# Attention stage of a decoder layer: order of the values, of one load of keys and of the query rows

## The chip, the cores and the metric

One core of a Trainium2 chip runs the whole layer in one launch. The time is device microseconds of that core; three runs of the kernel before gave 2487.85, 2491.16 and 2492.6 us. The core has TensorE (PE; PEld is its weight loads), VectorE (DVE), ScalarE (ACT), GpSimd (POOL) and SyncE (SP), which work side by side and wait for each other only where data or buffers demand it. In this kernel each engine runs its instructions in the order in which the program writes them.

## The reference

`x` is 16 sequences of 112 rows by 1024, the context 16 of 375 rows. Three blocks, each followed by a layer norm without weights:

```
x = layernorm(x + ((topk_zeroed(silu(x @ Wg.T)) * (x @ Wu.T)) @ Wd.T))  # the half with the smallest size zeroed
q = x @ Wq                        # 32 heads of 32
k, v = ctx @ Wk, ctx @ Wv         # 8 heads of 32, each shared by 4 heads of q
p = softmax(q @ k.T * 32 ** -0.5)
x = layernorm(x + (p @ v) @ Wo)
x = layernorm(x + bf16(x) @ bf16(dequantize(qweight, qscale, qzeros)).T)
```

## The kernel before

The first 1746 us compute the first block and the keys and values of the context; rows of `x` after the first norm go to DRAM as `x1_d`, keys and values as `k_d` and `v_d`. The rest, `attention_and_ffn` (L1247), is what the change touches.

Attention is cut into 128 **units** (L1541): a sequence `b` (16), a half `c` of the key heads (2) and a position `r` in the group of four heads that share one key head (4). A unit handles four heads at once. The loop at L1619 writes, for each unit `n`, these steps in this order:

- at every fourth unit the load of the keys for the next four units (L1621), by SP's queue;
- `scores(n)` (L1304): four matmuls of 32 rows into two PSUM tiles (`sc0`, `sc1`, one buffer each), two maxima on DVE (L1323), four exponentials on ACT (L1325). The next unit's scores need the PSUM tiles back from the exponentials;
- `normalize(n - 1)` (L1331): reciprocals on DVE, a product on POOL (L1334);
- `square(n - 2)` (L1338): a transposition in squares of 32 on DVE (L1345), and after each second unit 16 transfers of 96 KB that lay the weights out for the values, 11 on SP's queue and 5 on POOL's (L1359);
- one piece of other matmul work (L1630 to L1634): either a piece of a tail, or, where none is ready, a chunk of the queries of a coming group of two sequences (`Queries.chunk`, L1235: 8 products of 224 columns, copied out by ACT). A chunk is also taken ahead of tail pieces when its group comes near (`due`, L1630);
- at every even unit the values of the pair of units that ended five units before (`attend`, L1601, which calls `values`, L1361): 12 products, with one PSUM tile `po` per four units, copied to `aT` by ACT after its second pair, and then the load of the next values by SP;
- rows of a coming group (L1638 to L1647): `Queries.rows` (L1223) transposes 112 rows by 1024 on PE and ACT copies them into `x1T`; two sequences make a group, the second two units after the first, since both pass through one buffer `xr` that `fetch` (L1218) loads by ACT's queue. The eight chunks of the group come after both;
- `lights(n)` (L1597): steps of tails that hang on a unit: statistics, `normed` (L1450: normalization by ACT, a cast to bf16 by DVE), `turn` (L1455: transposes on PE, a copy by ACT), `store`.

A **tail** is a block of 128 rows whose attention is complete: `project` (L1403) multiplies by the output weights, in two halves of columns, each in two pieces; an add on DVE (L1415), statistics, the cast, the turn, and `packed` (L1463), the product with the dequantized weights, whose result POOL adds (L1474). Its rows `x1` (L1400) lie in one of three buffers. In both kernels the pieces of tails start after the values that complete their rows.

Before the loop (L1544 to L1551) SP issues the first keys, two loads of values, and the output weights in 16 transfers of 256 KB. After the loop (L1653 on) the last values, tails and the store follow in an order written out by hand.

The rule that says when the rows of the next group are due:

```python
due = (turned // GB - 1) * per_group if turned % GB == 0 else when + 2
if not asked and turned < B and n >= due:
```

`turned` counts sequences whose rows are transposed, `asked` holds the chunks that wait, `per_group` is 16 units, `GB` is 2 and `LAG` is 5.

Of the kernel before, what the change touches and what calls it, by code (L numbers as in the profile page):

```python
# [10 lines left out]
F32 = mybir.dt.float32  # L11
# [11 lines left out]
P = 128  # L23
B, S, D = 16, 112, 1024
NT = B * S
TT = NT // P
KC = D // P
# [10 lines left out]
GB = 2  # L38
# [24 lines left out]
LAG = 5  # L63
# [1146 lines left out]
class Queries:  # L1210
# [4 lines left out]
        self.pool = ctx.enter_context(tc.tile_pool(name="q_work", bufs=1, side="right"))  # L1215
        self.x1T, self.qT, self.xr = {}, {}, {}

    def fetch(self, queue, g, bb):  # L1218

        self.xr[g, bb] = self.pool.tile([S, D], F32, tag="xr", name=f"xr_{g}_{bb}")  # L1220
        queue.dma_start(self.xr[g, bb], self.x1_d[ds((g * GB + bb) * S, S), :])

    def rows(self, g, bb):  # L1223
# [23 lines left out]
def attention_and_ffn(nc, tc, ident, ident_b, negh, x1_d, k_d, v_d, queries, wf_sb, wo, out):  # L1247
# [16 lines left out]
    with ExitStack() as ctx:  # L1264
# [6 lines left out]
        ld = ctx.enter_context(tc.tile_pool(name="a_ld", bufs=2))  # L1271
# [21 lines left out]
        def load_keys(b, c):  # L1293
            keys[b, c] = ld.tile([P, SK], F32, tag="kT", name=f"kT_{b}_{c}")
            nc.sync.dma_start(keys[b, c], k_d[:, c, ds(b * SK, SK)])

        def load_values(b, c):
            vals[b, c] = ld.tile([P, NKP, P], F32, tag="v", name=f"v_{b}_{c}")
            nc.sync.dma_start(
                vals[b, c],  # L1300
                v_d[ds(b * SK, SKP), ts(c, P)].rearrange("(k p) n -> p k n", p=P),
            )

        def scores(n):  # L1304

            b, c, r = units[n]
            kt = keys[b, c]
            q = queries.qT[b // GB]
            pr = probs[:, n % 3]
            sums = small.tile([P, 4], F32, tag="sums", name=f"sums_{n}", bufs=4)  # L1310

            sc, nmax = [], []
            for h in range(2):
                sc.append(ps_s.tile([P, 2, 512], F32, tag=f"sc{h}", name=f"sc_{n}_{h}"))
                nmax.append(small.tile([P, 2], F32, tag=f"nmax{h}", name=f"nmax_{n}_{h}", bufs=2))
            for i in range(4):
                nc.tensor.matmul(  # L1317
                    sc[i // 2][:, i % 2, :SK],
                    q[ts(i, HD), c * REP + r, ds(b % GB * (GT - P), P)],
                    kt[ts(i, HD), :], start=True, stop=True,  # L1320
                )
            for h in range(2):
                nc.vector.tensor_reduce(nmax[h], sc[h][:, :, :SK], AX.X, ALU.max, negate=True)  # L1323
            for i in range(4):
                nc.scalar.activation(  # L1325
                    pr[:, i, :SK], sc[i // 2][:, i % 2, :SK], AF.Exp,
                    bias=nmax[i // 2][:, i % 2 : i % 2 + 1], accum_out=sums[:, i : i + 1],
                )
            return sums

        def normalize(n, sums):  # L1331
            pr = probs[:, n % 3, :, :SK]
            nc.vector.reciprocal(sums, sums)  # L1333
            nc.gpsimd.tensor_tensor(  # L1334
                pr, pr, sums.unsqueeze(2).to_broadcast([P, 4, SK]), ALU.mult
            )
# [205 lines left out]
        n_units = len(units)  # L1542
        per_group = n_units // (B // GB)
        load_keys(0, 0)  # L1544
        load_values(0, 0)
        load_values(0, 1)
        by_head = wo.rearrange("p (c i) n -> p i c n", i=4)
# [6 lines left out]

        asked, behind, light = deque((0, mc) for mc in range(EARLY, KC)), deque(), {}
        turned, fetched, when = GB, GB, 0
        sums, tails = {}, {}
        done = soon = now = 0

# [13 lines left out]
        def piece(n, halves=(0, 1)):  # L1573

            nonlocal now
            now = n
            if opened:
                close()
                return True
            i = next((i for i, (first, *_) in enumerate(behind) if first <= n), None)  # L1580
            if i is None:
                return False
            _, tail, part = behind[i]
            del behind[i]
            if part < 2:
                tail.project(part, 0)
                opened.append([tail, part, 0])
            else:
                tail.packed(halves)
                if halves == (0,):  # L1590
                    behind.append((n, tail, part))
                    return True
                at(n + 1, tail.stats)
                at(n + 2, tail.store)
            return True

        def lights(n):  # L1597
            for step in light.pop(n, []):
                step()

        def attend(m):  # L1601

            nonlocal soon, done
            b, c, r = units[m]
            while r == 3 and ((b + 1) * S - 1) // P - 3 in aTs:
                piece(n)
            values(m)
            if r == 3 and m // 4 + 2 < 2 * B:
                load_values(b + 1, c)
            if r == 3 and c == 0:  # L1610
                soon = (b + 1) * S // P
            while (c, r) == (1, 3) and (done + 1) * P <= (b + 1) * S:
                if done not in tails:
                    tails[done] = Tail(done)
                tail = tails.pop(done)
                behind.extend((n + 1, tail, i) for i in range(2))
                done += 1

        for n in range(n_units):  # L1619
            b, c, r = units[n]  # L1620
            if n % 4 == 1 and n // 4 + 1 < 2 * B:  # L1621
                load_keys(*divmod(n // 4 + 1, 2))
            sums[n] = scores(n)
            if n:
                normalize(n - 1, sums.pop(n - 1))
            if n > 1:
                square(n - 2)

            now = n
            due = asked and n >= asked[0][0] * per_group + asked[0][1] - 2  # L1630
            if due or (not piece(n) and asked):
                queries.chunk(*asked.popleft())
            if n == 0:
                queries.chunk(*asked.popleft())  # L1634
            if n > LAG and (n - LAG) % 2:
                attend(n - LAG)

            due = (turned // GB - 1) * per_group if turned % GB == 0 else when + 2  # L1638
            if not asked and turned < B and n >= due:
                when = n  # L1640
                queries.rows(turned // GB, turned % GB)
                turned += 1
                if turned % GB == 0:
                    asked.extend((turned // GB - 1, mc) for mc in range(KC))
            if fetched == turned < B:
                queries.fetch(nc.scalar, fetched // GB, fetched % GB)
                fetched += 1  # L1647
            lights(n)
            if done + len(tails) < soon and Tail.live < 3:
                tails[done + len(tails)] = Tail(done + len(tails))  # L1650


        n = n_units  # L1653
# [34 lines left out]
def kernel(  # L1688
# [37 lines left out]
    with AsWritten(nc, tc) as order:  # L1726
        with ExitStack() as psum:
# [30 lines left out]
            for mc in range(EARLY):  # L1758
                queries.chunk(0, mc)
        attention_and_ffn(nc, tc, ident, ident_b, negh, x1_d, k_d, v_d, queries, wf_sb, wo, out)  # L1760


# [46 lines left out]
```

## Time and profile before

| | us |
|---|---|
| three runs, median | 2491.16 |
| profiled execution, its own time | 2492.81 |
| its span in the profile | 2491.0 |
| first scores start (unit 0) | 1746.67 |
| last scores start (unit 127) | 2429.37 |
| last values start | 2457.35 |

PE counts as busy for 98% of the span, DVE 54%, POOL 45%, ACT 31%. The mean granted clock of TensorE is 0.991. Matmuls are pipelined and their ends are modelled, so a busy PE need not run at its best. In a line of the timeline the numbers are start, length and, after the shape, how many instructions were merged; a bracket gives the idle time of that engine before it and what ended it. In the table of stages each engine has its busy time and its count of instructions; after them stand the granted clock of TensorE, the busy share of the 16 DMA engines and GB/s.

### The profile page before, as it was taken

What the parts mean: (1) busy time and instruction counts of PE and PEld (TensorE: products, weight loads), DVE (VectorE), ACT (ScalarE), POOL (GpSimd) and SP (SyncE); (2) the same over time, 40 slices, a digit from 0 to 9 for tenths busy, and PEclk for the clock granted to TensorE, in tenths of its full rate; (3) what the DMA queues carried; (4) which work ended last, traced back from release to release, by engine and by line L of the source; (5) the groups of instructions that cost most, each with busy time, mean ns of one, the idle gap of its engine ahead of it and who ended that gap; (6) DMA issues with size and microseconds to landing.
All of it is one profiled execution on the core that took longest, in us unless ns stands there. A gap on an engine that the chain in (4) does not pass through costs nothing. (4 is left out here: it accounts for less than half of the span.)

```text
span 2491.0 us, 31025 instructions
## 1 busy us (share of the span) xinstructions
PE 2438.1 (98%) x9746; PEld 1373.1 (55%) x9746; DVE 1349.6 (54%) x2258; ACT 782.3 (31%) x1844; POOL 1108.7 (45%) x1086
## 2 busy tenths in 40 slices
PE   9999999999999999999999999999899999999997
PEld 4456666544445666666964444444655555565543
DVE  0283587698862333332311523167667777777773
ACT  0352354345520111111110000000555655555652
POOL 1756233244253242332310000033578888888883
PEclk9999999999999999999999999999999999999998
DMA  9567876855454978676765233275877777787763
GB/s 358 197 244 267 294 265 233 259 177 182 141 179 134 305 233 262 202 224 205 244 203 163 77 117 102 73 237 182 199 194 189 199 193 199 186 207 190 194 183 104
DMA packets 331082, 498.12 MB, mean 200 GB/s; under 512 B 49849, under 2 KB 264994, under 8 KB 329122
## 3 DMA queue, kind: packets, MB, share of 16 engines
q1 hardware_dynamic: 260770, 381.93, 49.9%
q0 software_dynamic: 23168, 61.66, 8.4%
q10 hardware_dynamic: 46976, 52.50, 6.7%
q8 instruction: 80, 1.31, 0.2%
q14 instruction: 88, 0.72, 0.1%
HBM read 311.64 MB, written 83.63 MB: 159 GB/s over the span
## 5 line engine op out<-in xcount | busy, mean ns | idle before, releaser
L1334 POOL TENSOR_TENSOR probs<-probs,sums 128x1500 f32<-128x1500 f32 x128 | 344.2, 2691 | 118.0 <-DVE sums L1333 102.8
L1325 ACT ACTIVATE probs<-sc,nmax 128x375 f32<-128x375 f32 x512 | 286.7, 572 | 230.0 <-DVE nmax L1323 224.2
L1323 DVE TENSOR_REDUCE nmax<-sc 128x2 f32<-128x750 f32 x256 | 228.6, 931 | 127.3 <-PE sc L1317 126.7
L1011 PE MATMUL m<-wd,h 128*128 128x512 f32 (+1 forms) x616 | 265.1, 592 | 0.0
L698 ACT ACTIVATE ja<-a,to 128x1824 int8<-128x1824 f32 x98 | 177.8, 1814 | 211.5 <-DVE to L758 198.2
L470 POOL TENSOR_TENSOR c<-c,us 128x384 f32<-128x384 f32 (+1 forms) x84 | 89.0, 1060 | 346.0 <-DVE c L418 148.0
L1345 DVE STREAM_TRANSPOSE squares<-probs 128x1536 f32<-128x1536 f32 x128 | 224.2, 1751 | 26.8 <-DMA weights<-squares 11.4
L406 PE MATMUL pu_A<-u,xe 128*128 128x384 f32 (+2 forms) x768 | 237.9, 453 | 0.0
L406 PE MATMUL pu_S<-u,xe 128*128 128x384 f32 (+2 forms) x768 | 237.8, 452 | 0.0
L406 PE MATMUL pu_S<-u,xl 128*128 128x384 f32 (+2 forms) x768 | 230.0, 453 | 0.0
L1240 PE MATMUL bank<-x1T,wq_sb 128*128 128x224 f32 x1008 | 209.9, 362 | 0.0
L1240 PEld LDWEIGHTS bank<-x1T,wq_sb 128*128 128x128 f32 x1008 | 188.0, 192 | 34.4 <-issue 30.7
L1011 PEld LDWEIGHTS m<-wd,h 128*128 128x128 f32 (+1 forms) x616 | 116.8, 190 | 146.1 <-issue 144.4
L1409 PE MATMUL bank<-wo_sb,aT 128*128 128x512 f32 x416 | 192.0, 605 | 0.0
L406 PEld LDWEIGHTS pu_S<-u,xe 128*128 128x128 f32 x768 | 145.8, 190 | 76.0
L1359 POOL DMA_DIRECT2D weights<-squares x320 | 178.9, 565 | 8.9 <-issue 4.4
L406 PEld LDWEIGHTS pu_S<-u,xl 128*128 128x128 f32 x768 | 143.7, 190 | 70.9
L406 PEld LDWEIGHTS pu_A<-u,xe 128*128 128x128 f32 x768 | 141.6, 190 | 65.6 <-issue 0.4
L502 ACT COPY hT<-pt 128x384 f32<-128x384 f32 (+1 forms) x112 | 47.7, 426 | 363.5 <-PE pt L498 331.4
L1141 POOL TENSOR_TENSOR y<-y,c 128x512 f32<-128x512 f32 x7 | 10.0, 1423 | 326.9 <-DMA zi<-in_qz_dram 326.8
L242 PE MATMUL pg<-wg_sb,xp 128*128 128x456 f32 (+1 forms) x384 | 149.9, 553 | 2.1 <-DMA wg_sb<-in_wg_dram 2.1
L1317 PE MATMUL sc<-kT,qT 32*128 32x375 f32 x1024 | 139.3, 533 | 11.0 <-ACT probs L1325 6.0
(204 smaller groups left out, 3391.3 us busy)
## 6 DMA issues: line engine op xcount, KB each, us to landing
weights<-squares SPq DMA_DIRECT2D x704, 96.0 KB
h<-hT_d SPq DMA_DIRECT2D x56, 640.0 KB
weights<-squares POOLq DMA_DIRECT2D x320, 96.0 KB, 3.5
xe<-in_xT_dram SPq DMA_DIRECT2D x48, 512.0 KB
xe<-xs_d SPq DMA_DIRECT2D x48, 512.0 KB
xl<-xs_d SPq DMA_DIRECT2D x48, 512.0 KB
u<-in_wg_dram SPq DMA_DIRECT2D x32, 688.0 KB
a<-s_d SPq DMA_DIRECT2D x14, 1376.0 KB
```

The lines of the kernel that those rows point to most:

```text
L242: nc.tensor.matmul(pg[:, :w], xts[t][:, kc, :], wg_sb[:, kc, ds(off, w)], start=(kc == 0), stop=(kc == KC - 1),)
L406: nc.tensor.matmul(m, a(n), k[:, n, :], start=(n == 0), stop=(n == KH - 1))
L698: nc.scalar.activation(ja, a[:, NV:], AF.Sign, bias=to, scale=-1.0, accum_out=st["sgn"])
L1011: self.nc.tensor.matmul(bank, a[:r, k, :], b(k)[:r], start=(k == 0), stop=(k == HK - 1),)
L1240: nc.tensor.matmul(pq[:, :GT], self.wq_sb[:, kc, ts(mc, P)], self.x1T[g][:, kc, :], start=(kc == 0), stop=(kc == KC - 1),)
L1317: nc.tensor.matmul(sc[i // 2][:, i % 2, :SK], q[ts(i, HD), c * REP + r, ds(b % GB * (GT - P), P)], kt[ts(i, HD), :], start=True, stop=True,)
L1323: nc.vector.tensor_reduce(nmax[h], sc[h][:, :, :SK], AX.X, ALU.max, negate=True)
L1325: nc.scalar.activation(pr[:, i, :SK], sc[i // 2][:, i % 2, :SK], AF.Exp, bias=nmax[i // 2][:, i % 2 : i % 2 + 1], accum_out=sums[:, i : i ...
L1334: nc.gpsimd.tensor_tensor(pr, pr, sums.unsqueeze(2).to_broadcast([P, 4, SK]), ALU.mult)
L1345: nc.vector.transpose(sq[:, :, n % 2].rearrange("p k (i f) -> p k i f", f=Q), probs[:, n % 3].rearrange("p i (k f) -> p k i f", f=Q),)
L1359: queue.dma_start(wt[ts(m, Q), :, j], by_part[ts(j, Q), :, m])
L1409: nc.tensor.matmul(self.pp, aT[:, h, r, :], wo_sb[:, h * REP + r, ts(i, 512)], start=(h == 0 and r == 0), stop=(h == 1 and r == REP - 1),)
```

## The change

Four things, all in the attention stage. The second keys are loaded right after the first, ahead of the 16 output-weight transfers, and no longer at unit 1. The values of a pair come one unit later, at odd units, right behind that unit's scores and ahead of its piece of other work, instead of at the end of the even unit. The second sequences of the groups 1 and 2 (numbers 3 and 5) have their rows loaded before the loop, into two of the three `x1` buffers, which no tail uses yet; their rows may be transposed in the same unit as the first sequence's. The rows of a group are due one unit earlier than before, and the rule may run twice in a unit.

```diff
-    def fetch(self, queue, g, bb):
-
-        self.xr[g, bb] = self.pool.tile([S, D], F32, tag="xr", name=f"xr_{g}_{bb}")
+    def fetch(self, queue, g, bb, place=None):
+
+        if place is None:
+            place = self.pool.tile([P, D], F32, tag="xr", name=f"xr_{g}_{bb}")
+        self.xr[g, bb] = place[:S]
         queue.dma_start(self.xr[g, bb], self.x1_d[ds((g * GB + bb) * S, S), :])
...
         load_keys(0, 0)
+        load_keys(0, 1)
         load_values(0, 0)
...
         turned, fetched, when = GB, GB, 0
+        apart = {GB + 1, 2 * GB + 1}
+        for i in sorted(apart):
+            place = ld.tile([P, D], F32, tag="x1", name=f"xr_{i}", bufs=3)
+            queries.fetch(nc.scalar, i // GB, i % GB, place)
...
-            if n % 4 == 1 and n // 4 + 1 < 2 * B:
+            if n % 4 == 1 and 1 < n // 4 + 1 < 2 * B:
                 load_keys(*divmod(n // 4 + 1, 2))
             sums[n] = scores(n)
+            if n > LAG + 1 and n % 2:
+                attend(n - LAG - 1)
...
-            if n > LAG and (n - LAG) % 2:
-                attend(n - LAG)
-
-            due = (turned // GB - 1) * per_group if turned % GB == 0 else when + 2
-            if not asked and turned < B and n >= due:
-                when = n
-                queries.rows(turned // GB, turned % GB)
-                turned += 1
+
+            for _ in range(2):
                 if turned % GB == 0:
-                    asked.extend((turned // GB - 1, mc) for mc in range(KC))
-            if fetched == turned < B:
-                queries.fetch(nc.scalar, fetched // GB, fetched % GB)
-                fetched += 1
+                    due = (turned // GB - 1) * per_group - 1
+                else:
+                    due = when + (0 if turned in apart else 2)
+                if not asked and turned < B and n >= due:
+                    when = n
+                    queries.rows(turned // GB, turned % GB)
+                    turned += 1
+                    if turned % GB == 0:
+                        asked.extend((turned // GB - 1, mc) for mc in range(KC))
+                if fetched == turned < B:
+                    if fetched not in apart:
+                        queries.fetch(nc.scalar, fetched // GB, fetched % GB)
+                    fetched += 1
```

## The prediction

> **What bounds the kernel now.** I read the page first, then the busy time of the engines by stage, then the matmul timeline of the attention stage unit by unit (a unit is one pass of the loop at L1619), then DVE and ACT beside it, and last the chain of waits at the end.
>
> ```profile
> PE 2438.1 (98%) x9746; PEld 1373.1 (55%) x9746; DVE 1349.6 (54%) x2258; ACT 782.3 (31%) x1844; POOL 1108.7 (45%) x1086
> ```
>
> TensorE is the bound over the whole, so only what makes it idle or slow can be won. The stages (start and end, length, busy time of PE, PEld, DVE, ACT and POOL, granted clock, DMA share, GB/s) are units 0 to 20, units 21 to 126, and the end:
>
> ```profile
> 1746.67:1858.69 112.02, 100.15 (x664) 72.42 (x665) 72.45 (x86) 60.66 (x198) 76.14 (x66) 0.91 0.80 195
> 1858.69:2429.37 570.68, 563.62 (x3612) 316.18 (x3609) 438.09 (x552) 330.41 (x1016) 474.08 (x442) 1.00 0.76 194
> 2429.37:2491.00 61.63, 44.05 (x194) 18.55 (x192) 23.38 (x41) 17.08 (x30) 21.17 (x25) 0.89 0.38 102
> ```
>
> The loss sits at both ends of the attention stage, where the clock is also below 1. The same view around the low clock:
>
> ```profile
> 1766.99:1770.40 3.41, 0.00 (x0) 0.00 (x0) 0.00 (x0) 0.00 (x0) 3.41 (x6) 1.00 1.05 222
> 1784.05:1787.46 3.41, 2.71 (x16) 1.37 (x16) 3.40 (x5) 2.32 (x10) 3.17 (x2) 1.00 1.09 258
> 1787.46:1794.29 6.83, 6.63 (x19) 4.61 (x20) 3.67 (x5) 4.46 (x16) 6.80 (x7) 0.50 1.08 240
> 1838.66:1848.90 10.24, 6.12 (x40) 3.13 (x40) 4.33 (x5) 2.86 (x9) 6.94 (x7) 0.50 1.08 247
> ```
>
> After a thin 3.4 us the clock is halved for 3.4 us or a few times that. The timeline of PE shows what is thin:
>
> ```profile
> 1762.96 3.29 PE L1240 MATMUL bank<-x1T,wq_sb 128*128 128x224 f32 x16
> 1770.44 1.75 PE L1317 MATMUL sc<-kT,qT 32*128 32x375 f32 x8 [4.18 <-DMA kT<-k_d]
> ...
> 1780.99 0.91 PE L1317 MATMUL sc<-kT,qT 32*128 32x375 f32 x8
> ...
> 1784.25 0.90 PE L1317 MATMUL sc<-kT,qT 32*128 32x375 f32 x4 [0.91 <-ACT probs L1325]
> 1785.36 0.90 PE L1317 MATMUL sc<-kT,qT 32*128 32x375 f32 x4 [0.21 <-ACT probs L1325]
> ...
> 1834.30 1.51 PE L1317 MATMUL sc<-kT,qT 32*128 32x375 f32 x8
> 1837.55 0.90 PE L1317 MATMUL sc<-kT,qT 32*128 32x375 f32 x4 [1.75 <-ACT probs L1325]
> ...
> 1844.40 2.79 PE L1372 MATMUL po<-weights,v 128*32 128x256 f32 x24 [4.12 <-DMA v<-v_d]
> ```
>
> Unit 4 waits for its keys. Scores wait for the exponentials of the unit before: the first half can start 3.26 us after the last scores (1780.99 to 1784.25), the second 1.11 us later. Filler must cover that. In dense rows scores take 0.84 us (start to next start), a query chunk 3.23, values 1.43, half a projection 3.63, row transposes 0.86, turning a tail 0.65, the packed product 3.56. Call excess what a unit lasts beyond its pieces. Units 0 to 20 have 24.5 us of it: 4.25 in unit 3 and 1.65 in unit 4 (half clock); 6.4 in units 6 to 8; 11.1 in units 16 to 18, 4.12 of it the last line above; the rest are splits of 0.28 after a unit of scores and one chunk (4.07 us, under the 4.37 after which the second half may go). Units 21 to 126 have about 20.
>
> A tail (projection, norm, turn, packed product) delays scores through DVE, whose cast waits for ACT and stands ahead of the next maxima:
>
> ```profile
> 1890.20 1.75 DVE L1453 CAST xb<-x 128x1024 bf16<-128x1024 f32 x1 [1.24 <-ACT x L1446]
> 1891.87 1.77 DVE L1323 TENSOR_REDUCE nmax<-sc 128x2 f32<-128x750 f32 x2
> ```
>
> And in the chain that ended last, the packed product's adds on POOL go ahead of the last normalization, and the last values run at half clock after a wait:
>
> ```profile
> 2438.29 2.27 POOL x L1474 x2
> 2440.57 2.64 POOL probs L1334
> ...
> 2454.94 2.17 DMA weights<-squares
> 2457.35 2.79 PE po L1372 x24
> 2460.14 3.41 PE bank L1467 x8
> ```
>
> **The change, units 0 to 20.** Followed through the loop's rules, the new order is: unit 5 turns both row blocks of group 1, chunks of group 1 fill units 6 to 13, unit 15 turns both of group 2. The keys of unit 4 go before 16 output-weight loads whose issue took 22.95 us (1741.04 to 1763.97), so unit 3 and 4 lose nothing but two splits. Units 6, 7, 16, 17 have a chunk each. Unit 14 has scores alone: 3.26 - 0.84 = 2.42 idle, and the split second half, done at 3.26 + 1.11 + 0.42 where dense work would have 3.26 + 0.84, adds 0.69: 3.1. Half a window of 3.4 us at half clock is 1.7; I take it at three chances in four: 1.3. Nine splits of 0.28 make 2.5. New excess 6.9, so **-17.6**.
>
> What hides the moved transfers: two row blocks (0.92 MB) now ride on ACT's queue beside the output weights. At the 235 GB/s of 1740 to 1760 that is 3.9 us, so SP issues the first weights to about 1775.8 instead of 1773.8 and they land by 1779; the first values (unit 7 now) want them near 1781. SP stood idle from 1774.4 to 1780.67, so later pairs catch up. ACT's two issues (0.33 us each) fall into the 3.09 us in which it waits for the first maxima. Were they held by a buffer or by the last x1 write (issued at 1748.96, median 3.8 us to land), the first exponentials would start near 1754 to 1759, not 1750.95. Before fetched rows at 1699.0 ahead of a later write on program order, so rows wait for their own writes alone: I take 0; the other end is +3 to +8.
>
> **Holes that move down.** All chunks now come earlier, and the fillers no longer reach everywhere. Unit 28 has scores and a turn, unit 52 the same, unit 84 scores alone, unit 125 scores and values. Unit 84: 3.1 + 1.3 - 0.28 = +4.1. Units 28 and 52: with values in front, the chunk of the unit before ends at 5.78; copy 0.36, normalize 1.25, cast 1.14 follow (means of their groups), so the two maxima start near 8.5 and end at 10.3, the exponentials at 11.8, the next scores at 12.4, against 7.8 of work (5.50 + 0.84 + 0.65 + 0.84): 4.6. Unit 52's predecessor also turns rows: 4.9. The old excess there was 1.8 and 1.5, so +2.8 and +3.4; a turn of 0.65 inside 5 us is surely a thin window, 1.8 each: +9.8 together. Unit 125: maxima wait for a cast and the statistics of another tail (DVE 1.25 + 0.36), and the last scores end 5.2 above work against 1.0 now; with 1.0 for the clock +5.2. Sum **+19.1**.
>
> **Values in front.** The same instructions. A pair's squares are done about 4.5 us into a unit; its values started 4.07 us into the third unit after (4.07 + 5.79 + 4.07 + 4.07 - 4.5 = 13.5) and now start 0.84 us into the fourth (5.5 + 4.35 + 5.5 + 4.35 + 0.84 - 4.5 = 16.0), so the three small waits on those DMAs (0.50, 0.55, 0.67) go; the packed product no longer waits 0.25 for its copy, since values stand between. What was covered by values at a unit's end (the chunk's copy, the adds) is bare: the cast comes 0.7 us later against the next scores. Tails 1, 2 and 4 to 9 had 1.8, 1.9, 2.6, 1.5, 2.7, 2.2, 0 and 1.0; by the same steps I get 1.2, 1.2, 1.2, 0.9, 0.6, 1.2, 1.1 and 0.6: -5.7; further splits and statistics +0.7. **-5.0**, bounds +3 (cover lost in each of eight tails at 0.7, waits gone) and -8.
>
> **The end.** Values 121 (1.43) and half a projection (3.63) now come after the last scores: 5.1 us less before them. After them PE has 1.43 + 3.63 + 3.56 + 7.2 + 1.43 + 0.65 + 7.06 + 1.43 + 0.7 = 27.1 us up to the last values, against 26.15 taken now (2431.2 to 2457.35), of which 3.55 is waiting. The last normalization no longer stands behind the adds: POOL is free 6.0 us after the scores, then 2.7 for it, 1.8 for the square and the 12.3 that now pass from the square's end (2445.0) to the values make 23: no wait, and the half clock (2.79 for 1.43, 3.41 for about 1.8) goes, 2.8. -5.1 + 0.95 - 2.8 = **-6.9**.
>
> **Sum:** -17.6 + 19.1 - 5.0 - 6.9 = -10.4. The profiled execution took 2492.81 (span 2491.0 and 1.8 around it), 1.65 above the median 2491.16. On the median: 2481.
>
> **A rule on the clock.** The row above shows half clock after 1784.05 to 1787.46, in which no gap was over 0.91 us and PE counted 2.71 of 3.41 busy. The Trainium skill, TensorE: Matmul & The Clock Gate (What's actually happening), gives half rate after at least one idle window of about 3.4 us. By it the holes of 2.4 us would cost no clock, and the sum, without its 7.2 us for that, would be -17.6. The row decides; this is no end of my range.
>
> **Rivals.** *Nothing at the end:* if POOL or SP still bring the last weights late, -6.9 is gone: -3.5, 2488. For it: SP issued 20 loads in 19.75 us there. *ACT held by the early rows:* +5, 2486; for it the late x1 write, against it the fetch at 1699.0. *Holes that deepen (slower):* if each of the five holes is followed not by one low window but by three, as at 1838.66 (10.24 us, 5.1 lost), each costs 3.7 more (5.1 less the 1.0 to 1.8 above): +18, 2499. It turns the sign over 0.2% from 3.1 more per hole. For it DMA at 1.08 share there, which delays values and feeds the hole; against it only one of three early holes went so far, and it had a wait of 4.12 in it. *Clock untouched by the holes:* -17.6, 2474.
>
> **Numbers.** A measurement here can tell about 0.2%, 5 us, from no change. Forecast 0.55, own range 2475 to 2487; end lost 0.13; ACT held 0.07; holes deepen 0.16; clock untouched 0.09. Of the forecast a tenth falls within 0.2%. Faster 0.61 (0.50 + 0.09 and a little of the second), same 0.23, slower 0.16. The range of 2473 to 2497 takes in all but the tips of the last two.
>
> **What would show it.** Right: no wait for kT at unit 4; no gap at units 6, 7, 16 to 18 and clock 1.00 from 1746 to 1800; gaps of 2 to 3 us with half clock after them at units 14, 28, 52, 84 and 125; no wait on weights before the last values. Wrong: ACT's first exponential after 1753; holes with ten low microseconds; a DMA wait ahead of values in units 7 to 19; the last values still waiting.

## The result and the profile after

The changed kernel is slower: 2504.0 us (median of six runs, 2500.59 to 2508.35) against 2489.99 for the kernel before in the same comparison, a ratio of 1.0058 with a 95% interval of 1.0043 to 1.0072. That is 14 us where 10.4 us less were forecast. Its profiled execution took 2504.43 us, span 2502.6; lines after the edits sit two or three further down (scores L1319, chunks L1242, values L1374, weights L1361).

The busy time on the page, then the three stages (units 0 to 20, units 21 to 126, the end) as before:

```profile
PE 2443.1 (98%) x9746; PEld 1376.2 (55%) x9746; DVE 1343.9 (54%) x2258; ACT 780.0 (31%) x1844; POOL 1110.8 (44%) x1086
```

```profile
1746.73:1859.20 112.47, 102.47 (x688) 78.19 (x688) 71.46 (x83) 60.86 (x200) 75.08 (x64) 0.95 0.80 192
1859.20:2438.05 578.85, 560.76 (x3553) 311.20 (x3553) 433.38 (x553) 327.85 (x1014) 474.88 (x442) 0.98 0.77 191
2438.05:2502.60 64.55, 49.15 (x224) 20.91 (x224) 23.85 (x41) 17.44 (x30) 21.38 (x25) 0.89 0.37 99
```

Work moved between the rows: three query chunks from the second to the first, one unit's values from the first to the second, and 5.06 us (one unit's values and half a projection) from the second to the third. With the prediction's excess (what a unit lasts beyond its pieces, at the prediction's prices), units 0 to 20 fell from 24.6 to 16.8, units 21 to 126 rose from 20.2 to 41.7, and the end, less the work that moved in, fell by 2.1: -7.8 + 21.5 - 2.1 = +11.6, which is what the span grew by (2491.0 to 2502.6).

**The early loss.** PE in units 6 and 7:

```profile
1777.11 3.29 PE L1242 MATMUL bank<-x1T,wq_sb 128*128 128x224 f32 x16
1780.34 1.19 PE L1319 MATMUL sc<-kT,qT 32*128 32x375 f32 x8
1787.69 2.79 PE L1374 MATMUL po<-weights,v 128*32 128x256 f32 x24 [6.16 <-issue]
```

The first values wait 6.16 us and then take 2.79 in place of 1.43: unit 7 alone has 8.43 of excess. The chain of waits names what came late, a row load, then SP, then weights:

```profile
1776.44 4.57 DMA xr<-x_d
1784.24 2.17 DMA weights<-squares
1786.41 1.27 issue
1787.69 2.79 PE po L1374 x24
```

SP's own view has the same load (who waited for what: total, times, longest), and its timeline shows 11 weights loads spread over 18.77 us where before they took 7.12:

```profile
SPq L1361 <- DMA xr<-x_d: 10.4, 1, 10.4
```

```profile
1766.72 18.77 SPq L1361 DMA_DIRECT2D weights<-squares  x11
```

The third row load (sequence 4) sits on ACT's queue, not on SP's. Why SP waits for it stands in the compiled instructions, where each lists the semaphores it waits for. SP's loads take eight completion semaphores (DMAHW0 to 7) in turn, and so do ACT's. The first line below is ACT's load of `xr_2_0`, the others are SP's. SP's numbers jump from 2 to 4 in the output weights (883 and 884), because ACT's load took number 3; the fifth load of the first weights (891) then has to wait for number 3:

```
858 L1223 DMACopy xr_2_0_11024<-x1_d_106 112x1024 [waits DMAHW3_49,DMAHW1_49]
...
882 L1554 DMACopy wo_sb_10729<-in_wo_dram 32x2x1024 [waits DMAHW1_49]
883 L1554 DMACopy wo_sb_10729<-in_wo_dram 32x2x1024 [waits DMAHW2_49]
884 L1554 DMACopy wo_sb_10729<-in_wo_dram 32x2x1024 [waits DMAHW4_49]
...
891 L1361 DMACopy weights_0_10895<-squares_0_10865 32x3x256 [waits DMAHW3_49]
```

ACT can issue that load only when the row transposes of unit 5 have freed its buffer; it did at 1776.44, the load landed at 1781.01, and SP went on at 1781.03. So a load on one queue held the other queue's loads by a shared number. SP needed neither its data nor its buffer: the section on the cores, which has engines wait only for those, left this out.

The same happened twice more, earlier. Among the output weights SP waited 14.3 us for row loads (8.5 for the early row block of sequence 3, then 5.8 for that of sequence 2), where the kernel before waited 10.5. In the first of these waits the DMA engines stood at a share of 0.64, in the one among the first weights at 0.92.

**The later loss.** Before, unit 28 held the packed product and values behind its second half of scores:

```profile
1895.28 0.90 PE L1317 MATMUL sc<-kT,qT 32*128 32x375 f32 x4 [0.21 <-ACT probs L1325]
1896.43 3.63 PE L1467 MATMUL bank<-wf_sb,x2T 128*128 128x512 bf16 x16 [0.25 <-ACT x2T L1461]
1899.98 1.50 PE L1372 MATMUL po<-weights,v 128*32 128x256 f32 x24
```

After, the hole at unit 28, then the stretch behind it in the windows view (last columns: granted clock, DMA share, GB/s):

```profile
1895.33 0.91 PE L1319 MATMUL sc<-kT,qT 32*128 32x375 f32 x8
1897.88 0.68 PE L1462 MATMUL bank<-ident_b,xb 128*128 128x128 bf16 x8 [1.64 <-DVE xb L1455]
1899.94 0.90 PE L1319 MATMUL sc<-kT,qT 32*128 32x375 f32 x4 [1.38 <-ACT probs L1327]
1901.05 1.62 PE L1319 MATMUL sc<-kT,qT 32*128 32x375 f32 x4 [0.21 <-ACT probs L1327]
1902.60 2.79 PE L1374 MATMUL po<-weights,v 128*32 128x256 f32 x24
1905.32 4.83 PE L1469 MATMUL bank<-wf_sb,x2T 128*128 128x512 bf16 x16
```

```profile
1901.00:1907.80 6.80, 6.75 (x34) 2.38 (x35) 3.68 (x5) 3.92 (x11) 5.32 (x5) 0.50 0.55 151
```

Excess: 7.4 in units 28 and 29, 7.4 in 52 and 53, 5.9 in 83 to 85, 4.0 in 125 and 126. Less what the same units had before, that is 6.0 + 6.5 + 5.7 + 4.0 = 22.2, more than the 21.5 of the whole stage, so its rest won 0.7.

**The end.** POOL's last weights loads, then PE up to the last values:

```profile
2458.84 2.76 POOL L1361 DMA_DIRECT2D weights<-squares  x5 [8.50 <-PE po L1374]
```

```profile
2457.01 1.50 PE L1374 MATMUL po<-weights,v 128*32 128x256 f32 x24
...
2469.82 0.70 PE L1462 MATMUL bank<-ident_b,xb 128*128 128x128 bf16 x8 [2.09 <-DVE xb L1455]
2470.51 2.37 PE L1374 MATMUL po<-weights,v 128*32 128x256 f32 x24
```

The loads want one of two weights buffers, which values 123, started at 2457.01, free only when they end; POOL stands before them for 8.50 us with the adds and the norm behind it, and the last turn waits for that norm's cast.

### The profile page after: what moved, and what is told of

It reads as the page before. It is cut to its first block, busy times and chain, and to the rows that moved or that the text cites. A ratio compares the mean times of both kernels' runs of the same rounds, so it can differ in the third digit from the quotient of the medians.

```text
span 2502.6 us, 31023 instructions
## 1 busy us (share of the span) xinstructions
PE 2443.1 (98%) x9746; PEld 1376.2 (55%) x9746; DVE 1343.9 (54%) x2258; ACT 780.0 (31%) x1844; POOL 1110.8 (44%) x1086
## 4 chain that ended last, share of the span: by engine, by line
PE 80%; DVE 8%; DMA 4%; ACT 3%; issue 2%; SPq 2%; POOL 1%; ACTq 0%; DVEq 0%; POOLq 0%
PE m L1011 18%; PE pu_S L406 18%; PE pu_A L406 13%; PE pg L242 6%; PE bank L1411 5%; PE bank L1242 5%; PE sc L1319 3%; PE po L1374 3%; SPq L1361 2%; PE pk_S L406 2%; ACT probs L1327 2%; DMA weights<-squares 1%; PE bank L1469 1%; PE pt L498 1%; PE pv_S L406 1%
## 5 line engine op out<-in xcount | busy, mean ns | idle before, releaser
L1347 DVE STREAM_TRANSPOSE squares<-probs 128x1536 f32<-128x1536 f32 x128 | 224.1, 1751 | 37.2 <-DMA kT<-k_d 15.6
L1242 PE MATMUL bank<-x1T,wq_sb 128*128 128x224 f32 x1008 | 209.4, 362 | 0.0
L1242 PEld LDWEIGHTS bank<-x1T,wq_sb 128*128 128x128 f32 x1008 | 187.7, 192 | 30.4 <-issue 28.4
L1361 POOL DMA_DIRECT2D weights<-squares x320 | 179.3, 566 | 15.0 <-PE po L1374 8.5
L1319 PE MATMUL sc<-kT,qT 32*128 32x375 f32 x1024 | 138.2, 529 | 14.8 <-ACT probs L1327 13.9
```

The lines of the kernel that those rows point to most:

```text
L1242: nc.tensor.matmul(pq[:, :GT], self.wq_sb[:, kc, ts(mc, P)], self.x1T[g][:, kc, :], start=(kc == 0), stop=(kc == KC - 1),)
L1319: nc.tensor.matmul(sc[i // 2][:, i % 2, :SK], q[ts(i, HD), c * REP + r, ds(b % GB * (GT - P), P)], kt[ts(i, HD), :], start=True, stop=True,)
L1347: nc.vector.transpose(sq[:, :, n % 2].rearrange("p k (i f) -> p k i f", f=Q), probs[:, n % 3].rearrange("p i (k f) -> p k i f", f=Q),)
L1361: queue.dma_start(wt[ts(m, Q), :, j], by_part[ts(j, Q), :, m])
```

## The experiments

All ratios are against the kernel before, with 95% intervals; 0.001 is 2.5 us.

### The three parts alone

Keys alone:

```diff
         load_keys(0, 0)
+        load_keys(0, 1)
...
-            if n % 4 == 1 and n // 4 + 1 < 2 * B:
+            if n % 4 == 1 and 1 < n // 4 + 1 < 2 * B:
```

> The kernel before with the second keys loaded early and nothing else. Theory A (a load on SP's queue waits for an earlier load with the same completion semaphore, and that one may sit on ACT's queue and not be issued yet): units 3 and 4 win 5.9 us, but now the fifth of the first pair's weights shares its semaphore with the row load that ACT issues only in unit 5. SP stands still for about 10 us (1770 to 1781), the first values wait about 6 us, and units 6 to 8 give back 4 to 8 us: -2 to +2 us against the kernel before. Rival B (the queues are independent, and what made the values late in the changed kernel was the bandwidth that two early row loads took): no early row loads here, so the whole 5.9 us less 0.6 for splits stay: -5 us.

1.0018 (1.0007 to 1.0028), +4.5 us. Units 3 and 4 won 5.6 of their 5.9, and units 6 to 8 lost 11.1. In SP's waits, the windows and PE's timeline:

```profile
SPq L1359 <- DMA xr<-x_d: 10.2, 1, 10.2
```

```profile
1775.00:1780.00 5.00, 4.88 (x36) 4.09 (x32) 3.62 (x5) 3.54 (x11) 4.66 (x3) 1.00 0.13 36
```

```profile
1789.89 2.79 PE L1372 MATMUL po<-weights,v 128*32 128x256 f32 x24 [10.01 <-DMA weights<-squares]
```

SP stood still from 1773.48 to 1783.70, and for five of these 10.2 us the DMA engines were nearly idle (share 0.13; 0.49 over the whole): no bandwidth can explain that. The compiled waits had shown it beforehand (`xr_1_1` had taken number 1, on which the fifth weights load waits). Theory A holds for the wait, but units 6 to 8 gave back 11.1, more than its 4 to 8, so the time lies above its -2 to +2.

Values alone, and rows alone (the changed kernel with keys and values as before):

```diff
             sums[n] = scores(n)
+            if n > LAG + 1 and n % 2:
+                attend(n - LAG - 1)
...
-            if n > LAG and (n - LAG) % 2:
-                attend(n - LAG)
```

> The kernel before with only the values moved one unit later, right behind the scores. The order then leaves unit 36 with scores and a turn and unit 125 with scores and values. Theory C (a unit without other work costs 3 to 5 us, and 1.8 to 3.5 more for the halved clock): +4 to +5 at unit 36, +5 at unit 125, 0 to -4 at units 6 to 18, -2 at the end, -3 to +3 in the other tails: about +4 us. Rival D (values in front cost nothing by themselves and remove small waits, as the prediction had it, -5 for the tails and -6.9 for the end): -3 us even with the two holes.

> The kernel before with only the row blocks moved (two early loads, both blocks in one unit, due one unit earlier); the values and the second keys as before. Thin units are 14 (scores, values), 15 (scores, two row blocks), 33 (scores, one row block) and 84 (scores, values). Theory A: the row load of group 2 shares its semaphore with a weights load of the third pair only, so the first values are not late; units 6 to 8 win 6.4, units 16 to 18 win 11.1 less about 4 for units 14 and 15, units 33 and 84 cost 3 each, units 3 and 4 keep their 5.9: -7 to -9 us. Rival B (early row loads cost bandwidth that delays the first weights): the 8 us of the changed kernel's unit 7 appear here too: about 0.

Values alone: 1.0056 (1.0039 to 1.0073), +14 us, more than either theory. The early units are nearly as before (22.4 of excess against 24.6); units 21 to 126 lost 16. PE at unit 36, which has nothing but scores and a turn:

```profile
1934.46 1.61 PE L1317 MATMUL sc<-kT,qT 32*128 32x375 f32 x8
1938.15 1.07 PE L1460 MATMUL bank<-ident_b,xb 128*128 128x128 bf16 x8 [2.07 <-DVE xb L1453]
1940.30 2.73 PE L1317 MATMUL sc<-kT,qT 32*128 32x375 f32 x8 [1.08 <-ACT probs L1325]
1942.97 2.79 PE L1372 MATMUL po<-weights,v 128*32 128x256 f32 x24
```

Units 36 and 37 have 8.4 of excess (0.3 before) and 10.3 us at a clock of 0.50 behind the hole (1937.60 to 1947.90); 125 and 126 have 4.25 (none before).

Rows alone: 1.0002 (0.9992 to 1.0013). That is B's number, but not by B's way: the first values do not wait. Units 0 to 20 won 6.3, although units 3 and 4 lose 9.9 there in place of 5.9 (SP waited 15.1 us for row loads among the output weights, and the second keys stand behind those); units 21 to 126 lost 5.9. A overlooked that the early loads hold SP themselves.

### What makes the first weights late

A third row block early, so that ACT issues none in unit 5:

```diff
-        apart = {GB + 1, 2 * GB + 1}
+        apart = {GB + 1, 2 * GB, 2 * GB + 1}
```

> The changed kernel with a third row block (sequence 4, the first of group 2) also loaded ahead of the loop, into the third x1 buffer, so that ACT issues no row load in unit 5. Theory A: nothing holds SP among the first pair's weights, the 6 us wait in unit 7 and its half clock go: -8 us against the changed kernel, some 6 us above the kernel before. Rival B (bandwidth of the early loads): 0.46 MB more ahead of the output weights, so the first weights come 2 us later still: +2 us against the changed kernel, 16 above the kernel before.

1.0051 (1.0037 to 1.0065): not told apart from the changed kernel. (Its profiled execution, 2510.7, was the slowest of six, with a median of 2503.26.) The hold among the first weights is gone from SP's waits, yet unit 7 still has 7.8 of excess (8.4 in the changed kernel). The line of SP's waits is what is left among the output weights:

```profile
SPq L1554 <- DMA xr<-x_d: 14.5, 2, 9.3
```

```profile
1745.00:1750.00 5.00, 4.51 (x27) 3.66 (x27) 4.21 (x9) 0.94 (x3) 0.76 (x2) 1.00 0.21 61
1780.00:1785.00 5.00, 3.32 (x20) 2.44 (x18) 0.87 (x2) 2.58 (x9) 3.40 (x3) 1.00 1.05 246
```

```profile
1788.31 2.79 PE L1374 MATMUL po<-weights,v 128*32 128x256 f32 x24 [5.00 <-DMA weights<-squares]
```

Now the DMA engines are full (1.03 to 1.05 from 1755 to 1785). So A misses here, and B's number is the nearer one: taking the hold among the first weights away, with 0.46 MB more loaded early, won nothing that can be told here. That the engines were busy during that hold in the changed kernel (0.92) fits. But bytes alone are not shown either. SP still waited 14.5 us for row loads among the output weights, and in the first of these waits the engines stood at 0.21 for five us, so part of what fills them later is work that was held back. This run does not tell the two apart. The Trainium skill, DMA: Bandwidth & Descriptors (Issuing engines are not separate DMA queues), says that loads issued by different engines run on the same 16 DMA engines and interleave. This run agrees: a row load by ACT took 11.5 us to land beside SP's output weights (1755.77 to 1767.24, share 1.03 to 1.05), and 4.57 in the changed kernel at 1776.44, with the share at 0.79.

The hold taken away in the kernel with the keys alone: only sequence 3 is loaded ahead of the loop (0.46 MB more), its transposition stays.

```diff
+        apart = {GB + 1}
+        for i in sorted(apart):
+            place = ld.tile([P, D], F32, tag="x1", name=f"xr_{i}", bufs=3)
+            queries.fetch(nc.scalar, i // GB, i % GB, place)
```

> The kernel with only the keys early, and in addition the row block of sequence 3 loaded ahead of the loop into an x1 buffer (its transposition stays where it was). Nothing that ACT issues in unit 5 then shares a completion with the first pair's weights. Theory A: SP no longer stands still for 10.2 us with the DMA engines at a share of 0.13; 0.46 MB more go ahead of the first weights (2 us); so of the 11.4 us in unit 6 some 6 to 8 go: -5 to -8 us against the kernel with only the keys early, -1 to -4 against the kernel before. Rival B (bytes alone): 2 us more, +2 against the kernel with only the keys early.

0.9994 (0.9985 to 1.0004): -6.0 us against the keys alone, as A said: there the hold among the first weights is a cause by itself. The wait is now 4.58 us, with the DMA engines full, again behind 15.6 us in which SP waited for row loads among the output weights:

```profile
1775.00:1780.00 5.00, 1.61 (x16) 0.86 (x14) 2.21 (x4) 3.71 (x13) 4.98 (x7) 1.00 1.06 227
```

```profile
1781.19 2.79 PE L1374 MATMUL po<-weights,v 128*32 128x256 f32 x24 [4.58 <-DMA kT<-k_d]
```

The output weights out of the way, in the kernel before, the changed kernel and the one with rows alone:

```diff
+        parts = deque((i, r) for i in range(4) for r in range(REP))
...
+            if n >= 2:
+                for _ in range(min(1, len(parts))):
+                    i, r = parts.popleft()
+                    nc.sync.dma_start(by_rep[ts(i, HD), r], by_head[ts(r, HD), i])
```

> The kernel before with the 16 output-weight loads issued one in each of units 2 to 17 in place of all ahead of the loop; nothing else is moved. Theory B (bytes ahead of the keys and the first weights): the second keys go out in unit 1 without a queue before them, so units 3 and 4 win 5.9 us, and the first weights find the DMA engines free. Theory A (shared completions) still holds SP: the tenth load of the second pair shares its semaphore with the row load that ACT issues only in unit 7, so the second values (unit 8) come late and 3 to 6 of the 6.4 us of units 6 to 8 stay. Together -6 to -9 us, about 2483. Rival: the spread loads delay the weights of later pairs by what they no longer delay at the start: -2 to +2.

> The changed kernel with the 16 output-weight loads issued one in each of units 2 to 17. Theory B: 3.9 MB less ahead of the first weights, and no weights of the first pair share a completion with a row load that is not issued: the wait of 6.2 us in unit 7 and its half clock go, -8 us against the changed kernel, about 6 above the kernel before. Rival: the first values are late because the squares or the scores are (DVE or ACT behind), whatever the loads do: no change, 14 above the kernel before.

> The kernel with only the rows moved, and the output-weight loads one in each of units 2 to 17. Theory B with holes (C): its 9.9 us of waits in units 3 and 4 go; units 14 and 15 (about 4), 34 (3) and 84 (1.4) stay: -8 to -10 us against the kernel with only the rows moved, and as much against the kernel before, about 2482. Rival: once units 3 and 4 no longer wait, the first values are asked for earlier and wait in their place (in the changed kernel this took all that the early keys won): -2 to 0.

In this order 1.0040 (1.0027 to 1.0053), 1.0076 (1.0062 to 1.0090) and 1.0023 (1.0014 to 1.0032): all three expectations of a gain were wrong. B was right about the place and wrong about the sum. In the changed kernel unit 7 no longer waits (0.28 of excess), but later pairs do, as PE's timeline shows:

```profile
1782.94 1.50 PE L1374 MATMUL po<-weights,v 128*32 128x256 f32 x24
...
1794.94 1.50 PE L1374 MATMUL po<-weights,v 128*32 128x256 f32 x24 [2.08 <-issue]
...
1838.58 2.79 PE L1374 MATMUL po<-weights,v 128*32 128x256 f32 x24 [3.87 <-issue]
```

Units 0 to 20 kept 18.3 of excess (16.8 in the changed kernel). In the kernel before, units 3 and 4 won 5.6, and units 6 to 8 and 16 to 20 lost 13.9. The 4 MB have to pass in units 0 to 20 anyhow, a stage with a DMA share of 0.80.

### What the holes cost

Spare products, whose result nobody reads, in the five holes of the changed kernel; 12 in each, then 6:

```diff
+            if n in (14, 28, 52, 84, 125):
+                spare = bank()
+                for _ in range(12):
+                    nc.tensor.matmul(spare[:, :GT], queries.wq_sb[:, 0, :P], queries.qT[b // GB][:, 0, :], start=True, stop=True)
```

> The changed kernel with 12 products of 128 by 224 (2.4 us) whose result nobody reads added in each of its thin units 14, 28, 52, 84 and 125, in the place of the missing other work. Theory C (a thin stretch is followed by half clock, and that is part of its cost): the waits for the exponentials stay, but the clock stays at 1.00 after them; the half clock is worth 1.7 us a window, so -1.7 for units 14, 84 and 125 and -1.7 to -3.4 for 28 and 52: -8 to -12 us against the changed kernel. Rival (what follows a hole is late because DVE and ACT are, and the clock plays no part): nothing is won, and added products that reach past the waits cost up to 1 each: 0 to +5.

> The changed kernel with 6 spare products in each of units 14, 28, 52, 84 and 125. (The 12 of the run before took 4.81 us, since each counts as two instructions and a chunk of 8 takes 3.23, not the 2.4 that its expectation said; 6 take 2.4.) Theory C: the idle of the five holes is 2.4 to 3.5 us each, so 6 products lie in it for nothing and the clock still stays up: each hole costs 1 to 2.4 less than with 12, -5 to -10 us against that run, about 2490. Rival (the clock needs the whole hole filled): the half clock comes back behind some holes, 1.7 each: within 2 us of the run with 12, or slower.

With 12: 1.0023 (1.0014 to 1.0032), 8.7 us faster than the changed kernel, though the 12 products took 4.81 us each time, 24 us in all (the expectation's 2.4 was wrong by a factor of two). Unit 28 in it, and the windows behind:

```profile
1898.53 4.81 PE L1642 MATMUL bank<-qT,wq_sb 128*128 128x224 f32 x24
1903.17 0.65 PE L1462 MATMUL bank<-ident_b,xb 128*128 128x128 bf16 x8
1903.76 0.91 PE L1319 MATMUL sc<-kT,qT 32*128 32x375 f32 x8
1904.60 1.50 PE L1374 MATMUL po<-weights,v 128*32 128x256 f32 x24
```

```profile
1903.00:1908.00 5.00, 5.00 (x52) 2.54 (x51) 3.82 (x5) 3.63 (x12) 3.05 (x2) 1.00 0.75 164
```

The clock stays at 1.00 behind all five, and units 28 and 29 last 11.9 us in place of 14.75. But not all of the 8.7 us is placed: in the profiled execution, 5.5 us faster than that of the changed kernel, the holes at 28 and 52 give 4.9 and the other three cost 1.6, and units 36 and 37, which got no products, have 2.5 more excess, with 3.4 us at 0.50. With 6: 1.0032 (1.0019 to 1.0044), not faster than with 12. Behind units 14 and 28 the clock stayed up, at no cost; behind 52 it fell, and at 84 the values waited 2.22 us for weights and the clock fell. The expectation of 5 to 10 us more failed, its rival is nearer.

The kernel before with such products in its own thin units (8 in units 3 and 18, 6 in 7 and 17, 2 in 6):

> The kernel before with spare products in its own thin units: 8 in units 3 and 18 (3.2 us, beside the waits of 4.2 and 4.1 for the second keys and for values), 6 in 7 and 17, 2 in 6. Theory C: half clock lasted 20 us in units 4 to 18 there (1771 to 1774, 1787 to 1794, 1839 to 1849), which is 10 us of work lost; with the idle filled most of that goes, while the waits themselves stay: -5 to -9 us against the kernel before, which makes it faster than both kernels. Rival (half clock follows from something else, such as the DMA engines at a share over 1): the clock falls as before and the spare products add up to 3 us: 0 to +3.

0.9991 (0.9981 to 1.0002): about -2, less than expected and not told from nothing. In its profiled execution units 4 and 8 ran at full clock, 5.3 us less, and units 0 to 20 as a whole won just those 5.3; the timed runs show less than half of it.

### The end

```diff
+        attend(n - 5)
         step(n)
-        attend(n - 5)
```

> The changed kernel with values 123 ahead of the packed product of tail 11 and the projection of tail 12 at the end, instead of behind them. Theory E (the last weights wait for a weights buffer that values 123 free, and POOL with them): POOL's last five loads no longer wait 8.5 us, the last values start 3 to 5 us earlier: -3 to -4 us against the changed kernel. Rival (the last normalization or the DMAs set the last values): the packed product is 1.4 us later and nothing is won: 0 to +1.5.

1.0068 (1.0053 to 1.0083): nothing won, as its rival said. (The profiled execution, 2501.98, was the fastest of six, with a median of 2508.43.) The wait on POOL did shrink, but values 123 now wait for their own weights, and from the last scores (2435.90) to the last values pass 33.8 us, 32.5 in the changed kernel:

```profile
2451.29 2.76 POOL L1361 DMA_DIRECT2D weights<-squares  x5 [3.10 <-DMA weights<-squares]
```

```profile
2447.28 1.71 PE L1374 MATMUL po<-weights,v 128*32 128x256 f32 x24 [2.67 <-DMA weights<-squares]
...
2469.73 1.50 PE L1374 MATMUL po<-weights,v 128*32 128x256 f32 x24
```

So the buffer is one of two limits there that lie close together; the other is when values 123 themselves have their weights.

### Where the values cost

Values in front up to unit 21 only, in the changed kernel and alone; and the changed kernel with the values as before:

```diff
-            if n > LAG + 1 and n % 2:
+            if LAG + 1 < n < 22 and n % 2:
                 attend(n - LAG - 1)
...
+            if n >= 22 and (n - LAG) % 2:
+                attend(n - LAG)
```

> The changed kernel with the values right behind the scores only up to unit 21 and in their old place from unit 22 on. Theory F (the values in front cost nothing early and 13 us later: tail pieces start a unit later, units 28, 52, 84 and 125 lose the values that filled them, and two pieces more are left at the end): units 28 and 52 fall from 7.4 to about 4 each, 84 from 5.2 to about 2, 125 from 4.0 to 0, the end is as before: -10 to -14 us against the changed kernel, about 2492. Rival G (the holes come from the chunks taken earlier, and where the values stand matters little): -2 to -4.

> The kernel before with the values right behind the scores up to unit 21 only, nothing else moved. Theory F: units 0 to 20 as with the values moved throughout (2 us less than before), unit 36 has scores, values and a turn (2 to 3 us), the rest and the end are as before: within 2 us of the kernel before, -11 to -14 against the values moved throughout. Rival (the cost sits in the early units, where other transfers meet the values): +8 to +13.

> The changed kernel with the values in their old place throughout (keys and rows as changed). Theories A, B and F: the row load that ACT issues in unit 5 shares its completion with the sixth of the first pair's weights, so unit 6 waits 7 to 9 us and eats most of the 9.9 that units 3 and 4 no longer lose; units 14, 15, 34 and 84 cost 5 more than before; no cost at 28, 52 and 125: -3 to +1 against the kernel before. Rival (the parts add up as measured alone: keys +4.6, rows -0.2): +4.4.

In this order 1.0006 (0.9997 to 1.0015), 0.9981 (0.9972 to 0.9991) and 1.0005 (0.9995 to 1.0015). One condition on `n` takes back 13 us of the 14, and so does leaving the values where they were. Theory F holds, G falls; the second run won 4.7 us where F gave it 2 at most. The hole at unit 28 in the first of them, with values in it and the old end of the stage:

```profile
1896.08 1.50 PE L1374 MATMUL po<-weights,v 128*32 128x256 f32 x24 [0.68 <-issue]
1897.52 0.71 PE L1462 MATMUL bank<-ident_b,xb 128*128 128x128 bf16 x8
1898.76 0.90 PE L1319 MATMUL sc<-kT,qT 32*128 32x375 f32 x4 [0.54 <-ACT probs L1327]
```

Excess there: 4.7 at units 28 and 29, 3.6 at 52 and 53, 2.0 at 84 and 85, none at 125; up to unit 126 it is 41.1 in all, where the changed kernel has 58.5. The third run has no holes at 28, 52 and 125; it keeps 9.0 in unit 6, 5.6 in 33 and 34 and 2.0 in 84 and 85.

### Versions that beat both

Keys and row 3 early, with spare products (10 in unit 6, 4 in 7, 6 in 17, 8 in 18); then keys, row 3 early and values in front to unit 21, without and with spare products (8 in unit 6, 6 in each of 16, 17, 18 and 36):

> The kernel with the early keys and the early row block of sequence 3, and spare products in its thin units: 10 in unit 6, 4 in 7, 6 in 17, 8 in 18. Theory C: the waits of 4.6 and 4.1 us for weights stay but are no longer followed by half clock (1.4 in unit 6, 1.4 in 18, some tenths behind them): -2 to -4 us against the kernel without the spare products, -4 to -6 against the kernel before, the fastest of all. Rival: as in the run with 6, the clock falls all the same and the spare products cost: 0 to +3 against the kernel without them.

> The kernel before with early keys, the row block of sequence 3 loaded ahead of the loop, and the values right behind the scores up to unit 21. By F and A: the first values are asked for a unit later (0.84 us into unit 7 in place of unit 6's end), so the wait of 4.6 us there shrinks to about 2; units 3 and 4 keep their 5.9: -3 to -5 us against the kernel before by adding -1.4 and -3 to -5. Rival: the values to unit 21 paid because units 3 and 4 were late, and without that wait nothing more is won: about -1.5.

> The same with spare products in its thin units: 8 in unit 6, 6 each in 16, 17, 18 and 36. Theory C: another -2 to -4 us, 6 to 8 below the kernel before. Rival: spare products that reach past the idle cost as much as the clock gives: within 1.5 us of the run without them.

In this order 0.9984 (0.9975 to 0.9993), 0.9971 (0.9957 to 0.9985) and 0.9960 (0.9946 to 0.9973): 2488.4, 2484.0 and 2484.1 us. The joined versions are 7 to 10 us faster than the kernel before and some 20 faster than the changed one. The first of them has 36.9 of excess up to unit 126 (44.8 before). What the spare products add to it is not measurable: the intervals overlap and the medians are equal.

## Why the prediction was wrong

By its own terms, in us, measured in the two profiled executions (the medians differ by 14):

| term | predicted | measured |
|---|---|---|
| units 0 to 20 | -17.6 | -7.8 |
| holes at 28, 52, 84, 125 | +19.1 | +22.2 |
| rest of units 21 to 126 | -5.0 | -0.7 |
| end | -6.9 | -2.1 |
| sum | -10.4 | +11.6 |

**Units 0 to 20: the step on moved transfers failed.** "SP issues the first weights to about 1775.8 ... and they land by 1779" priced the moved row loads by their bytes alone, and took SP's queue to be free of ACT's. SP issued the last of them at 1785.5, 9.7 us later: row loads of ACT's queue held it for 14.3 us among the output weights and for 10.4 among the first weights, and unit 7 lost 8.4. That a hold alone can do this is shown in the kernel with keys alone (10.2 us held, and 6.0 us won when the hold went). In the changed kernel 5.00 of the 6.16 us of wait were left when that hold went and 0.46 MB more were loaded early; how much bytes and how much the holds among the output weights make of it is open. The prediction looked for a hold by the early rows, but on ACT, where it did not come (its first exponential starts at 1748.75); it came on SP. Units 3, 4, 6, 8 and 16 to 18 behaved as forecast, 14 with 15 cost 5.1 (4.4 forecast), and 19 waited 1.3 more for its weights.

**The holes: right in place, nearly right in size, half right in cause.** They were put to "all chunks now come earlier". That is one half. The other is the values, which end a tail's attention a unit later and leave the units before without that tail's pieces. At 28 and 52 it takes both: rows alone leave 1.4 and 0.3 of excess there, values alone 1.0 and 0.2, the two together 7.4 each. The hole at 125 comes with the values alone (4.25), and 84 with 85 has 2.0 without them and 5.2 with them. The values cost about the same in either setting: +14 alone, 13 on top of keys and rows. So the two terms that were credited to them (-5.0 and -6.9) and most of the +19.1 belong to one edit. Booked together they would have been +7 even at the predicted sizes, and the sign hung on the start alone.

**Half clock behind holes: right at four of five.** It was taken from one row against a rule. The Trainium skill, TensorE: Matmul & The Clock Gate (What's actually happening), asks for a whole idle window of about 3.4 us. After unit 84, gaps of 2.34 and 0.21 us were followed by 3.4 us at 0.50, after unit 28 gaps of 1.64, 1.38 and 0.21 by 6.8:

```profile
2209.70:2215.00 5.30, 2.75 (x22) 0.99 (x24) 4.32 (x5) 3.05 (x10) 5.28 (x7) 1.00 0.94 230
2215.00:2218.40 3.40, 3.40 (x28) 1.73 (x29) 2.84 (x4) 2.92 (x10) 3.26 (x2) 0.50 1.09 209
```

The run with 12 spare products shows that it is the idle that does it, and the rule as stated is not what decided here. How much idle it takes stays open: gaps of 1.55 and 0.21 behind unit 125 were followed by no half clock, the next ones (1.38 and 0.21 at the last scores) were, from 2440.3 to 2443.7, which counts to the end. The rival "clock untouched" is out; "holes that deepen" had the right sign, but there were two low windows at 28 and 52 and one at 14 and 84, not three each (with the values alone it was three, behind unit 36).

**The end: the step on POOL failed.** "No wait" overlooked that the last pair's weights need the buffer that values 123 free, and that these now stand behind 15.8 us of other pieces after the last scores. 4.8 of the 6.9 were lost there. The rival "nothing at the end" named POOL bringing the last weights late, and that is what the profile shows; but the run with values 123 first did not get the 4.8 back, so the wait on POOL is not the only cause.

**What stays open.** Why the values to unit 21, alone, win 4.7 us: its profiled execution took 2491.1 us, above its median of 2489.0, and has only 2.5 us less excess than the kernel before up to unit 126. And what fraction of the holes is clock and what is idle: the runs with 12 and with 6 products are not told apart.

## What to carry to other kernels

Before a load is moved, read in the compiled waits on which earlier load each following one waits, across queues: a load that cannot be issued yet stopped another queue that shared its number, and its price was not its bytes alone. Where PE is dense, a step that is moved to a later unit also moves everything that depends on it; list unit by unit what is left in each, and price an empty unit at its idle plus a half-clock window or two. A gain in one unit counts only as far as the next transfer is early enough.

## What the runs showed of the hardware

Useless products made a kernel faster: 24 us of them, in five holes, took 8.7 us off, and the clock, which had fallen to 0.50 behind four of the holes, stayed at 1.00 behind all five. SP stood still for 10.2 us, five of them with the DMA engines at a share of 0.13, for a load of another queue. A row load of 448 KB landed 11.5 us after issue beside output weights in the run with three early rows (1755.77 to 1767.24), at a DMA share of 1.03 to 1.05.
